# Four due times of a hand-written timetable: a transform's first step by 0.14, the last transform by 0.12

## The chip, the cores and the metric

The kernel runs on one core of one Trainium2 chip. The metric is the device time of one execution in microseconds. The kernel before takes 3285.62 us, the median of three runs (3276.33 to 3288.96).

## The reference

The input is a batch of 32 images of 56 x 56 tokens with 96 channels, in float32. Two layers follow one another.

```python
# layer 0: layer norm over channels, product to 192, 3x3 convolution back to 96
h = (x - mu) * rsqrt(var + 1e-5) * ln_w + ln_b
x1, z = split(einsum('bhwc,cd->bhwd', h, w_in) + b_in, 2)
x = x + silu(conv3x3(x1, conv_w) + conv_b)
# layer 1: the 3136 tokens of an image mixed in the frequency domain
h = relu(bn1(einsum('bnc,hc->bnh', ln(t), w1)))
X = fft(h, axis=tokens)
xr = relu(X.real * rd - X.imag * idg + rb)
xi = relu(X.imag * rd + X.real * idg + ib)
t = t + bn2(einsum('bnh,ch->bnc', ifft(xr + 1j * xi).real, w2))
# and a two-layer network on values quantised to eight bits, accumulated in 16
t = t + q(relu(q(ln(t) @ W1.T + b1)) @ W2.T + b2)
```

## The kernel before

An image's 3136 tokens lie as 112 partitions of 28 tokens. They go in 7 groups of 4 tokens a partition (index g) or in four chunks of 8, 8, 8 and 4 (index i). The convolution works on a copy of the image in channels by position (make_image), with six combined rows in place of three (conv_part in three parts, conv_first, conv_last), and its output returns to tokens (conv_tokens, conv_end).

The Fourier transform of length 3136 = 112 x 28 is done in two steps. The first, over 112, is a matmul for each pair of tokens: tokens_a turns a group to channels, forth multiplies by w1 (tile ph, line 209, then the relu into tile h, line 212), forth_a applies the transform (tile pa, line 218, copied to tile u). store_a writes u to a scratch in DRAM, da, and fetch_a reads it back in another layout, tile at. The second step, over 28, is second (tile px, line 233, one matmul for each pair of frequencies; index m is one of four units of frequencies and u a part of the channels). Three activations of px give av (lines 238 to 240); second_parts makes sv on VectorE (lines 249 to 252) and second_relus makes gt (lines 258 and 259). The way back is second_w2 (tile pg), second_back (tile pe, copied to es), store_back (es to a second scratch, de), fetch_y (de to tile y), back (tile py, line 294) and back_end, which adds py to the tokens on VectorE (line 474) and, for every second group, takes the statistics of the next layer norm. The quantised network follows: normal, ffn_start, ffn_first three times (tile pf, line 305), ffn_middle (lines 315 and 316), ffn_second (tile po), ffn_end and store.

Work of several images runs at once. Each step of each image gets a due time in a timetable: plan(b) puts it at 8 * b plus a number, so that a new image starts every 8 units, and steps of several images interleave. The list is sorted by due time and the steps are emitted in that order. The program is built with a scheduler that follows the order of emission as a preference (line 848): each engine's own order is fixed when the program is built, from what the scheduler reckons to be ready, so a step can overtake one that is due earlier. On the chip each engine works through its own list, and an instruction that waits holds those behind it. All DMAs named here are issued from one queue, that of SP.

The PSUM tiles ph, px and py share one tag, "c", with two buffers (lines 207, 227 and 293); pa, pg, pe and po share another, "b", also with two. The tag "a" of pf has one.

The due times that matter, taken modulo 8 so that steps of neighbouring images stand beside each other: second(0, 0) of an image at 0.00; ffn_first(5, 1), of the image two before it, at 0.13; forth(0, 0) of the next image at 0.15; a part of its convolution, conv_part(2, 1), at 0.20; back(0) of the image before at 0.38; ffn_first(5, 2) at 0.41; forth_a(0, 0) at 0.42; conv_tokens(3) at 0.45; ffn_start(6) at 0.50; back_end(0) at 0.53; ffn_middle(5, 2) at 0.58; conv_end(3) at 0.60; second(0, 1) at 0.62. From line to line they come from these numbers of plan: FIRST for the first transform, BACK for the last one, FFN for the network; second has its own list of offsets (line 572), and fetch_y is due at the later of BACK - 0.6 and 2.9 before its back.

Of the kernel before, what the change touches and what calls it, by code (L numbers as in the profile page):

```python
# [80 lines left out]
def hybrid_kernel(ctx: ExitStack, tc: tile.TileContext, x, par, spar, w_in, conv_w, w1, w2, fw1, fb1, fw2, fb2, fa, fb, ib, ia, rows6, out):  # L81
# [437 lines left out]
    def plan(b):  # L519
        im = Image(b)  # L520

        def put(when, f, *args):
            order.append((8 * b + when, len(order), lambda: f(im, *args)))

        for i, (j0, j1) in enumerate(LN_CHUNKS):
            last = i == len(LN_CHUNKS) - 1

            at = CONV - 8 + 2 * (i + 1)
            ats = (-0.95, -0.7) if last else (0.2, 0.5, 0.85) if i == 2 else (0.25, 1.0, 1.5)
            put(at + ats[0] - (2.5 if b else 12), fetch, i)  # L530
            put(at + ats[0] - 1.15, take_in, i)
            for part, j in enumerate(range(0, j1 - j0, 3)):
                put(at + ats[part], make_image, i, j, min(3, j1 - j0 - j))

            at = CONV + 2 * i
            put(at + 0.6, im_load, i)
            ats = (0, 0.35, 0.7) if last else (0, 0.5, 1.25)
            for part in range(3):
                put(at + ats[part], conv_part, i, part)
            put(at + ats[1] + 0.2, conv_first, i)  # L540
            put(at + ats[2] + 0.2, conv_last, i)
            for g, off in zip(range(j0 // G4, j1 // G4), (1.85, 2.75)):
                put(at + off, conv_tokens, g)
                put(at + off + 0.15, conv_end, g)
            put(FIRST + 2 * i - 0.75, deviation, i)
        put(CONV - 0.6, make_seam)
        for g in range(NG):
            at = FIRST + g
            put(at - 0.35, tokens_a, g)
            for j2 in range(2):  # L550
                put(at + 0.15 + 0.6 * j2, forth, g, j2)
                put(at + 0.42 + 0.58 * j2, forth_a, g, j2)
            put(at + 1.2, store_a, g)
            at = BACK + g
            put(max(BACK - 0.6, at - 2.9), fetch_y, g)
            put(at, back, g)
            put(at + 0.15, back_end, g)
            at = FFN + g
            put(at - 0.7, normal, g, 0)
            put(at - 0.55, normal, g, 2)  # L560
            put(at - 0.35, ffn_start, g)
            for k in range(3):
                put(at + 0.28 * k, ffn_first, g, k)
                put(at + 0.28 * k + 0.17, ffn_middle, g, k)
            put(at + 1.0, ffn_second, g)
            put(at + 1.15, ffn_end, g)
            put(at + 1.5, store, g)
        for g in range(NS):
            put(max(FIRST + 7.4, g - (1.4 if g % 2 else 2.2)), fetch_a, g)
        for m, (p0, p1) in enumerate(UNITS):  # L570
            both = p1 - p0 > PG
            for at, u in ((0, 0), (0.62, 1), (1.25, 2)) if both else ((0, 0), (0.62, 2)):
                at += 2 * m
                put(at, second, m, u)
                put(at + 0.22, second_parts, m, u)
                put(at + 0.42, second_relus, m, u)
            for j0 in range(0, (p1 - p0) // 2, 2):
                at = 2 * m + (2 if both else 1.3) + 0.2 * j0
                put(at, second_w2, m, j0)
                put(at + 0.2, second_back, m, j0)  # L580
                put(at + 0.4, store_back, m, j0)
# [1 line left out]
    def im_load(im, i):  # L583
        im.load(i)

    CONV, FIRST, BACK, FFN = -12.3, -8, 8.38, 10.85
    for b in range(nb):
        plan(b)
    order.sort(key=lambda step: step[:2])
# [262 lines left out]
```

## Time and profile before

| what | value |
|---|---|
| median of three runs | 3285.62 us |
| the profiled execution | 3286.24 us |
| its span, first to last instruction | 3284.5 us |
| mean granted TensorE clock | 0.985 |
| TensorE matmul busy | 3178.5 us, 97% |
| VectorE busy | 2527.3 us, 77% |
| ScalarE busy | 2202.5 us, 67% |
| GpSimd busy | 573.4 us, 17% |
| issue to landing, median: da, at, de, y | 3.4, 4.7, 2.2, 2.8 us |

The profile is of one execution. Busy times are of each engine over the whole span. In the views of instructions each line is: start in us from the span's first instruction, duration in us, engine and line, operation, written tile and read tiles, shapes, how many were merged, and in brackets the idle time of the engine just ahead and what ended it. One matmul in float32 leaves two records. A row of the view of waits names an engine and line, what it waited for, the us in total, how many times, and the longest.

### The profile page before, as it was taken

The page shows a single profiled execution, that of the slowest core. Times are in us where ns is not written, and L with a number is a line of the kernel's source. Part 1 is how long each engine was busy: PE and PEld are TensorE (multiplying, and loading weights), DVE is VectorE, ACT ScalarE, POOL GpSimd, SP SyncE. Part 2 cuts the span into 40 slices and gives each one's busy share as a digit, 9 for nine tenths or more (in the row PEclk, how much of TensorE's full clock was granted, in tenths as well). Part 3 has the DMA queues.
Part 4 walks back from the last instruction along what each step waited for, and adds up shares of the span by engine and source line. Part 5 has one row for each costly group of instructions (what it writes and reads, how often), then busy time and mean ns, then how long its engine had stood idle before and what let it go on. Part 6 is the DMA issues. An engine that isn't in the chain of part 4 may idle for free.

```text
span 3284.5 us, 66741 instructions
## 1 busy us (share of the span) xinstructions
PE 3178.5 (97%) x23701; PEld 2732.7 (83%) x23701; DVE 2527.3 (77%) x7829; ACT 2202.5 (67%) x5232; POOL 573.4 (17%) x397
## 2 busy tenths in 40 slices
PE   7999999999999999999999999999999999999997
PEld 6888888888888888888888888888888888888875
DVE  4558777777878777877877777777777778777787
ACT  2566666766766666766666766667767666666776
POOL 1211111111211111112111111111111111121111
PEclk8999999999999999999999999999999999999997
DMA  4343334434344333344333344343344333443341
GB/s 109 94 116 98 104 110 123 120 99 112 94 118 120 109 107 105 106 117 119 111 102 109 107 117 123 96 112 104 110 123 119 100 103 101 120 118 99 104 117 55
DMA packets 334551, 355.45 MB, mean 108 GB/s; under 512 B 129304, under 2 KB 287400, under 8 KB 333992
## 3 DMA queue, kind: packets, MB, share of 16 engines
q1 hardware_dynamic: 332210, 349.01, 37.7%
q8 instruction: 188, 3.08, 0.4%
q10 hardware_dynamic: 2008, 2.17, 0.2%
q14 instruction: 145, 1.19, 0.1%
HBM read 196.93 MB, written 154.14 MB: 107 GB/s over the span
## 4 chain that ended last, share of the span: by engine, by line
PE 88%; DMA 7%; DVE 2%; ACT 1%; issue 1%; SPq 1%; POOL 0%; ACTq 0%; DVEq 0%; POOLq 0%
PE cv L164 22%; PE px L233 9%; PE pa L218 9%; PE ph L209 9%; PE im L153 7%; PE pg L276 5%; PE pe L286 5%; PE tp_n L146 5%; PE pg L272 5%; PE py L294 5%; PE pf L305 4%; PE po L322 3%; DMA de<-es 2%; PE st L196 2%; DMA at<-da 2%; DMA y<-de 1%
## 5 line engine op out<-in xcount | busy, mean ns | idle before, releaser
L164 PE MATMUL cv<-img,wv 97*96 97x224 f32 (+1 forms) x4608 | 882.4, 332 | 0.2
L164 PEld LDWEIGHTS cv<-img,wv 97*96 97x96 f32 x4608 | 662.0, 164 | 93.2 <-issue 11.2
L138 POOL TENSOR_TENSOR rs_c<-var_c,mhalf 112x8 f32<-112x8 f32 (+1 forms) x128 | 195.0, 1523 | 1679.7 <-DVE var_a L136 868.9
L212 ACT ACTIVATE h<-ph,rs_b 112x192 f32<-112x192 f32 x896 | 332.3, 429 | 177.5 <-PE ph L209 176.2
L233 PEld LDWEIGHTS px<-fb_sb,at 112*64 112x64 f32 (+1 forms) x3584 | 324.7, 165 | 132.7 <-issue 48.9
L233 PE MATMUL px<-fb_sb,at 112*64 112x112 f32 (+3 forms) x3584 | 381.9, 274 | 35.1 <-DMA at<-da 34.1
L307 ACT CAST h<-pf 128x448 f16<-128x448 f32 x672 | 363.8, 541 | 67.8 <-PE pf L305 64.5
L209 PE MATMUL ph<-w1a,n2t 97*112 97x192 f32 x1792 | 373.7, 328 | 4.1 <-DVE sv L252 2.8
L218 PE MATMUL pa<-h,fa_sb 112*112 112x384 f32 x896 | 365.6, 490 | 0.0
L138 POOL TENSOR_TENSOR rs_b<-var_b,mhalf 112x8 f32<-112x8 f32 (+1 forms) x128 | 190.4, 1488 | 984.7 <-DVE var_a L136 552.1
L153 PE MATMUL im<-rows_sb,xa 112*97 112x168 f32 x1792 | 325.2, 312 | 11.0 <-DVE xa L372 9.8
L488 DVE TENSOR_SCALAR xn<-t,st_c,rs_c 112x96 f32<-112x96 f32 x896 | 232.2, 325 | 111.3 <-POOL rs_c L138 108.7
L249 DVE SCALAR_TENSOR_TENSOR sv<-px,spar_sb,av 128x224 f32<-128x224 f32 (+2 forms) x352 | 153.4, 436 | 200.2 <-ACT av L240 199.3
L209 PEld LDWEIGHTS ph<-w1a,n2t 97*112 97x112 f32 x1792 | 290.7, 177 | 17.4 <-DVE sv L252 3.3
L153 PEld LDWEIGHTS im<-rows_sb,xa 112*97 112x97 f32 x1792 | 268.0, 167 | 43.2 <-issue 14.7
L219 ACT COPY u<-pa 112x384 f32<-112x384 f32 x448 | 215.4, 481 | 120.8 <-PE pa L218 111.5
L316 DVE CAST hq<-h 128x448 fp8e5<-128x448 f16 x672 | 257.9, 384 | 11.3 <-ACT h L313 5.4
L315 DVE TENSOR_SCALAR h<-h,b1q 128x448 f16<-128x448 f16 x658 | 215.4, 327 | 59.2 <-ACT h L307 54.4
L305 PE MATMUL pf<-n3t,w1q 96*128 96x448 fp8e5 x672 | 243.8, 363 | 9.6 <-ACT h L307 8.8
L276 PE MATMUL pg<-w2x,gt 128*112 128x96 f32 (+1 forms) x1792 | 251.6, 261 | 0.0
L238 ACT ACTIVATE av<-px,spar_sb 128x224 f32<-128x224 f32 (+2 forms) x352 | 156.7, 445 | 135.3 <-PE px L233 132.5
L276 PEld LDWEIGHTS pg<-w2x,gt 128*112 128x112 f32 (+1 forms) x1792 | 242.7, 179 | 0.2
(115 smaller groups left out, 6148.1 us busy)
## 6 DMA issues: line engine op xcount, KB each, us to landing
da<-u SPq DMA_DIRECT2D x224, 336.0 KB, 3.4
at<-da SPq DMA_DIRECT2D x224, 336.0 KB, 4.7
de<-es SPq DMA_DIRECT2D x448, 84.0 KB, 2.2
y<-de SPq DMA_DIRECT2D x224, 168.0 KB, 2.8
out<-o SPq DMA_DIRECT2D x224, 168.0 KB, 2.4
xl<-in_x SPq DMA_DIRECT2D x96, 336.0 KB, 3.4
x<-in_x SPq DMA_DIRECT2D x96, 336.0 KB, 4.1
xl<-in_x SPq DMA_DIRECT2D x32, 168.0 KB, 2.3
```

Of the source, the lines that this page charges most:

```text
L138: nc.gpsimd.tensor_tensor(rs, var, mhalf[:, :n], ALU.pow)
L153: nc.tensor.matmul(ps[:, j], xa[:, j, :], rows6_sb, start=True, stop=True)
L164: nc.tensor.matmul(ps[:, at], wv[:, k, dx, :], cols, start=(dx == 0), stop=(dx == 2))
L209: nc.tensor.matmul(ph[:, j, :], n2t[:, 2 * j2 + j, :], w1a, start=True, stop=True)
L212: nc.scalar.activation(h[:, j], ph[:, j], AF.Relu, scale=rs[:, 2 * j2 + j : 2 * j2 + j + 1])
L218: nc.tensor.matmul(pa, fa_sb, h, start=True, stop=True)
L233: nc.tensor.matmul(px[rows, j], lhs, fb_sb[:, first(p) : first(p + 1)], start=True, stop=True)
L276: nc.tensor.matmul(pg[:, half, j, :], lhs, w2x, start=False, stop=True, skip_group_check=True)
L305: nc.tensor.matmul(pf, w1q[:, k * 128 : (k + 1) * 128], n3t, start=True, stop=True)
L307: nc.scalar.copy(h1, pf)
L316: nc.vector.tensor_copy(hq[:, k, :], h2, saturate=False)
L488: nc.vector.tensor_scalar(xc[:, j], im.t[i][:, at, :C], mu[:, at : at + 1], rs[:, at : at + 1], ALU.subtract, ALU.mult)
```

## The change

Two numbers of plan change. second(0, 0) of each image, with its second_parts and second_relus, is due 0.14 later (the other second steps stay). BACK goes from 8.38 to 8.5, so that every back, back_end and fetch_y of every image is due 0.12 later. No instruction is added, removed or altered.

```diff
             for at, u in ((0, 0), (0.62, 1), (1.25, 2)) if both else ((0, 0), (0.62, 2)):
-                at += 2 * m
+                at += 2 * m + (0.14 if m + u == 0 else 0)
                 put(at, second, m, u)
                 put(at + 0.22, second_parts, m, u)
                 put(at + 0.42, second_relus, m, u)
@@
-    CONV, FIRST, BACK, FFN = -12.3, -8, 8.38, 10.85
+    CONV, FIRST, BACK, FFN = -12.3, -8, 8.5, 10.85
```

## The prediction

> **What bounds the kernel now.** I read first the page's busy times and its chain, then the waits of TensorE, then TensorE, the DMA queue and VectorE instruction by instruction around one image boundary (1306 to 1334 us). From the page:
>
> ```profile
> PE 3178.5 (97%) x23701; PEld 2732.7 (83%) x23701; DVE 2527.3 (77%) x7829; ACT 2202.5 (67%) x5232; POOL 573.4 (17%) x397
> ...
> PE 88%; DMA 7%; DVE 2%; ACT 1%; issue 1%; SPq 1%; POOL 0%; ACTq 0%; DVEq 0%; POOLq 0%
> ```
>
> TensorE is busy for 97% and carries 88% of the chain; the other thing in the chain is DMA, 7%. So only two things can move the time: TensorE's work, which the change leaves as it is, and the stalls between. TensorE's waits, longest first (total us, times, longest):
>
> ```profile
> PE px L233 <- DMA at<-da: 34.1, 32, 2.5
> PE py L294 <- DMA y<-de: 15.6, 18, 2.5
> ...
> PE py L294 <- ACT n2t L202: 2.7, 6, 0.5
> ```
>
> One px wait an image (34.1 us in all). The py waits come to 21.2 us over 28 times with the smaller rows of py (named for ScalarE work that had long ended, so I put them to y as well). TensorE at one boundary (start us, us, idle before):
>
> ```profile
> 1309.08 0.58 PE L164 MATMUL cv<-img,wv 97*96 97x224 f32 x2
> 1310.71 1.15 PE L233 MATMUL px<-fb_sb,at 112*128 112x114 f32 x8 [1.04 <-DMA at<-da]
> 1311.69 0.35 PE L305 MATMUL pf<-n3t,w1q 96*128 96x448 fp8e5 x1
> 1311.89 0.81 PE L209 MATMUL ph<-w1a,n2t 97*112 97x192 f32 x4
> 1312.54 2.06 PE L164 MATMUL cv<-img,wv 97*96 97x224 f32 x10
> 1314.43 0.49 PE L196 MATMUL st<-ident,s 96*112 96x96 f32 x4
> 1314.76 0.55 PE L146 MATMUL tp_n<-ident,t 112*97 112x112 f32 x4
> 1315.15 0.35 PE L305 MATMUL pf<-n3t,w1q 96*128 96x448 fp8e5 x1
> 1316.05 0.87 PE L294 MATMUL py<-y,ia_sb 113*112 113x384 f32 x2 [0.55 <-DMA y<-de]
> 1316.76 0.81 PE L218 MATMUL pa<-h,fa_sb 112*112 112x384 f32 x2
> ```
>
> These are second(0, 0) of one image (the px line) and back(0) of the image before it (the py line): exactly the steps that move. Between them stand one ffn_first, a forth, ten of the twelve records of a conv_part (a float32 matmul leaves two), a conv_tokens, a tokens_a and another ffn_first. The next boundary's px starts at 1409.70, so 8 units of the timetable are 98.99 us and one is 12.4 us: +0.14 is 1.7 us and +0.12 is 1.5 us. The order shown is the same at every boundary from 711 to 2903 us. In the DMA queue:
>
> ```profile
> 1306.91 1.26 SPq L428 DMA_DIRECT2D at<-da  x3
> 1308.26 0.88 SPq L459 DMA_DIRECT2D de<-es  x2
> 1313.63 1.25 SPq L465 DMA_DIRECT2D y<-de  x3
> ```
>
> Both chains (da to at, de to y) begin with TensorE work that stands before px, so the two arrival times don't depend on where px and py stand.
>
> [...]the 84 KB of de land in 2.2 us at the median, the 336 KB of at in 4.7[...]. [...]here both bubbles name a DMA. [...]in the dense stretch each next start lies 0.16 before the end shown, so the true stalls are 0.16 longer than the brackets (1.20 and 0.71 above). [...]whatever stands behind a waiting px or py waits too.
>
> **The change, part by part.** No instruction is added or removed.
>
> *Due time and place.* A due time is a preference, not a place: ffn_start(6), due at 0.50, runs before px, due at 0.00. But the tiles px, ph and py share two PSUM buffers, and their first matmuls start in the timetable's order all 1,024 times. Their due order (px 0.00, ph 0.15, py 0.38, px 0.62) becomes 0.14, 0.15, 0.50, 0.62: the same. So neither step can pass a ph or another px.
>
> *second(0, 0), +0.14.* The only TensorE step due between 0.00 and 0.14 is ffn_first(5, 1), at 0.13; now it stands right behind px. If it goes ahead, 0.20 us (1311.69 to 1311.89) fill part of the px stall of 1.20. But py then waits for y at the same moment, 1316.05, and the work between is the same set: TensorE is back 0.20 earlier and waits 0.20 longer. Worth 0 where y is late, up to 0.20 where it is not. Its three av activations (0.45 to 0.54 each) and three sv operations pass at most the h and hq of ffn_first(5, 1) (0.33 + 0.38 on VectorE), and the gt pair passes conv_first's; px's buffer may come free some 0.7 later. Who waits for it is the next px, 1317.45, against sv's end at 1314.43: 3.0 us of cover. I cost it at nothing; without the cover it is 0.7 an image. gt's first reader is second_w2 at 2.00, twenty us on.
>
> *back, +0.12 (seven an image).* It passes ffn_first(5, 2) at 0.41 and conv_tokens and ffn_start at 0.45 and 0.50, which run ahead already, and forth_a(0, 0) at 0.42: the pa line, which stands right behind py. Was pa ready? Its h ended at 1314.27 (0.76 from 1313.51 on ScalarE), 1.8 before py. Why was it not ahead, then? In the planner's order py and pa come as a pair: at back(0), (1), (3) and (5) the next matmul is that image's pa, at each of 24 boundaries that I went through. py(1) there waits for no DMA. What py (a free buffer) and pa (its input) share is the end of the h activations, which free ph's buffer and complete h; so I take it that both become ready at once and the due time decides. 0.42 against 0.38 put pa second; against 0.50 it is first. The price of pa is 1317.41 - 1316.76 = 0.65 us, in a stall of 0.71: gain 0.65 here. Summed, with min(0.65, bracket + 0.16) for each of the 25 py stalls over 0.3 between 312 and 3006 us: 20 at 0.65, and 0.64, 0.61, 0.54, 0.53, 0.48: 15.8 us. The other boundaries had no py stall. At (1), (3) and (5) the swap is worth 0: no stall there.
>
> *back_end, +0.12.* On VectorE it passes behind ffn_middle at .58 and, for g = 0, 2 and 6, conv_end at .60 (0.56 + four times 0.27 + 0.16 = 1.8 us); for g = 1 take_in at 1.60. This holds py's buffer longer. The next ph(0, 1) starts 3.8 us after the t of back_end(0): cover. The tightest is g = 1, in the rivals.
>
> *fetch_y, +0.12.* On the DMA queue the only step passed is fetch_a(2), 7.80: the first three fetch_y are due at 7.90 instead of 7.78. The three at already run ahead (1306.91 against 1313.63), and y waits for de till 1313.6. Nothing; if it were issued behind one more at, 0.4 us. The later y fetches pass no other DMA. A fetch_y(5) that waits for py(1), now 0.65 later, holds the queue by as much: its y is needed 50 us later.
>
> *Tail.* The last image has no successor whose pa could fill in; back stands alone. 0, at most 1.5 us.
>
> Sum: 3286.24 (3284.5 span + 1.74 around it) - 15.8 = 3270.4. The profiled execution lies 0.62 above the median, so 3269.8 there; I say 3270.
>
> **The rivals.**
> - *Nothing changes (3286).* If pa becomes ready in the planner's eyes only while py runs (up to 0.65 later also gives the order seen), py stays ahead; moving px alone is worth nothing. For it: px's stall stays, since hardly anything is due before 0.14. Against it: the pairing at four places.
> - *Both waits go (3236).* If the planner's order also closes the px stalls, 34.1 + 32 x 0.16 = 39, and with 15.8 some 55, less 5 for the first and the last image: 3236; with half of px's, 3253. Against it: conv_part's rest (0.20) and ph (0.15) are still due after px.
> - *A held buffer makes it slower (3313).* Place: back(1). Its t runs on VectorE at 1332.28 to 1332.83, though py ended at 1328.98, and the px that needs the buffer, second(1, 0), starts 0.29 later. VectorE, then TensorE:
>
> ```profile
> 1332.28 0.55 DVE L474 TENSOR_TENSOR t<-py,t 112x384 f32<-112x384 f32 x1
> ```
>
> ```profile
> 1328.17 0.81 PE L294 MATMUL py<-y,ia_sb 113*112 113x384 f32 x2
> 1328.82 0.81 PE L218 MATMUL pa<-h,fa_sb 112*112 112x384 f32 x2
> ...
> 1333.12 1.04 PE L233 MATMUL px<-fb_sb,at 112*128 112x112 f32 x8
> ```
>
>  The delay of t lies between 0.38 (only the hq of ffn_middle and a var slip ahead: 0.30 + 0.08; the statistics of take_in run ahead already) and 2.06 (pa 0.65, ffn_middle 0.71, take_in 0.70). Less 0.29, TensorE stands 0.1 to 1.8 us an image: 3 to 55 us over 31, or 3273 to 3325 with the gain. It decides from a delay of 1.33 on, a net loss of 16 us; the middle of what lies above is 3313. Against it: TensorE has other work, and the planner can put it ahead of px.
>
> **How the numbers follow.** pa ahead of py: 0.43, 3262 to 3279 alone. Nothing changes: 0.20, 3280 to 3292. Both waits: 0.13, 3236 to 3262. Slower: 0.24, 3302 to 3325. 0.5% is 16.4 us, about what a measurement of this kernel can tell (three runs of it spread over 12.6): faster is below 3269.2, slower above 3302. The likeliest case stands at that edge; with the spread I count 0.19 of its 0.43 as faster. Faster 0.19 + 0.13 = 0.32, same 0.24 + 0.20 = 0.44, slower 0.24. Range 3246 to 3318: it leaves out some 0.06 below and 0.08 above.
>
> **What would show it.** In the changed trace pa should stand before py at the boundary, and py's brackets for y fall from 21.2 to about 6 us; px's stay near 34. ffn_first before px with the px bracket at 0.84 and py's longer would bear out the fixed arrival. The prediction is wrong if py still comes first, if a new wait (px L233 for a VectorE t at second(1, 0)) appears, or if at or y land at another distance from the px before.

## The result and the profile after

The changed kernel takes 3246.83 us (3242.14 to 3251.24, four runs) against 3284.72 for the kernel before beside it: ratio 0.9888, 95% interval 0.9863 to 0.9912. That is 37.9 us less, where 14 to 16 were forecast; it lies 0.8 us above the foot of the range (3246). The profiled execution has a span of 3245.6 us, 38.9 below the one shown before.

The page of the changed kernel, busy times and chain by engine:

```profile
PE 3167.5 (98%) x23701; PEld 2737.2 (84%) x23701; DVE 2529.4 (78%) x7829; ACT 2196.2 (68%) x5232; POOL 598.2 (18%) x397
...
PE 87%; DMA 7%; DVE 3%; ACT 1%; issue 1%; SPq 0%; POOL 0%; ACTq 0%; DVEq 0%; POOLq 0%
```

The instruction counts are the same to the last one, and DMA still has its 7%: nothing was saved in work. TensorE's waits in the changed kernel (us in total, times, longest):

```profile
PE px L233 <- DMA at<-da: 19.3, 27, 2.7
...
PE py L294 <- DMA y<-de: 8.3, 15, 2.0
```

Both waits fell: py's from 21.2 us (all its rows) to 8.7, and px's for at, which was expected to stay near 34, to 19.3. TensorE at one boundary of the changed kernel (start us, us, idle before):

```profile
2569.45 0.78 PE L153 MATMUL im<-rows_sb,xa 112*97 112x168 f32 x4
2570.07 0.26 PE L146 MATMUL tp_n<-ident,xn 112*96 112x112 f32 x1
2570.16 0.54 PE L164 MATMUL cv<-img,wv 97*96 97x224 f32 x2
2570.96 1.15 PE L233 MATMUL px<-fb_sb,at 112*128 112x114 f32 x8 [0.25 <-DMA at<-da]
2571.94 0.82 PE L209 MATMUL ph<-w1a,n2t 97*112 97x192 f32 x4
2572.59 0.35 PE L305 MATMUL pf<-n3t,w1q 96*128 96x448 fp8e5 x1
2572.79 2.06 PE L164 MATMUL cv<-img,wv 97*96 97x224 f32 x10
2574.68 0.49 PE L196 MATMUL st<-ident,s 96*112 96x96 f32 x4
2575.01 0.45 PE L146 MATMUL tp_n<-ident,xn 112*96 112x112 f32 x3
2575.30 0.81 PE L218 MATMUL pa<-h,fa_sb 112*112 112x384 f32 x2
2576.41 0.90 PE L294 MATMUL py<-y,ia_sb 113*112 113x384 f32 x2 [0.30 <-DMA y<-de]
```

pa stands before py, as forecast. But px has no more work ahead of it than before: the same single matmul of the convolution (two records) stands in front, and ffn_first went behind ph instead of ahead of px. Its wait is shorter because at came sooner. The DMA queue at that boundary:

```profile
2561.03 0.33 SPq L364 DMA_DIRECT2D xl<-in_x  x1
...
2564.45 0.30 SPq L422 DMA_DIRECT2D da<-u  x1
2567.32 1.25 SPq L428 DMA_DIRECT2D at<-da  x3
```

From the last da store to the first at it is 2.87 us here. In the kernel before, the load xl of 336 KB was issued 0.65 us ahead of that store and the at followed 3.60 us after it; here the load is 3.4 us ahead. Followed through the boundaries of images 4 to 28 (means, before and after, us):

| stretch | before | after |
|---|---|---|
| end of the last pa of an image to the issue of its da | 1.48 | 1.29 |
| that issue to the first at | 3.85 | 3.12 |
| first at to px | 3.60 | 3.63 |
| sum, from pa to px | 8.93 | 8.04 |
| bracket of px | 1.10 | 0.49 |
| TensorE work between (sum less bracket less 0.16) | 7.67 | 7.39 |
| end of the last pe to py, the y chain | 9.22 | 8.01 |

The chain to px is 0.89 shorter and the work between is 0.28 less, so 0.61 of the wait is gone. The y chain is shorter as well: de is issued behind the three at, and these go out sooner. Three of the 25 boundaries before had y landed well ahead of py, so that the 9.22 is not all chain; without them it is 8.98, and the chain is about 1.0 shorter.

Where the 37.3 us went that 24 periods (from px of image 4 to px of image 28) became shorter: px stalls 13.2, py stalls 10.6, other stalls -1.0; 7.0 in the part of a period without stalls, 97.11 us before and 96.82 after (the median of a period less its stalls); and the remaining 7.5 mostly in slow stretches of TensorE, at a granted clock of 0.50, that the kernel before has four times and the changed one not at all in these periods. The last two are taken up below. Ahead of these periods 1.0 us was gained, behind them 0.6.

### The profile page after: what moved, and what is told of

The parts are those of the page before. It is cut to its first block, busy times and chain, and to the rows that moved or that the text cites. A ratio compares the mean times of both kernels' runs of the same rounds, so it can differ in the third digit from the quotient of the medians.

```text
span 3245.6 us, 66513 instructions
## 1 busy us (share of the span) xinstructions
PE 3167.5 (98%) x23701; PEld 2737.2 (84%) x23701; DVE 2529.4 (78%) x7829; ACT 2196.2 (68%) x5232; POOL 598.2 (18%) x397
## 4 chain that ended last, share of the span: by engine, by line
PE 87%; DMA 7%; DVE 3%; ACT 1%; issue 1%; SPq 0%; POOL 0%; ACTq 0%; DVEq 0%; POOLq 0%
PE cv L164 21%; PE px L233 9%; PE ph L209 9%; PE pa L218 8%; PE im L153 7%; PE tp_n L146 5%; PE pg L276 5%; PE pe L286 5%; PE pg L272 5%; PE py L294 4%; PE pf L305 4%; PE po L322 4%; DMA de<-es 2%; PE st L196 2%; DMA at<-da 2%; DMA y<-de 1%
## 5 line engine op out<-in xcount | busy, mean ns | idle before, releaser
L164 PEld LDWEIGHTS cv<-img,wv 97*96 97x96 f32 x4608 | 671.3, 164 | 101.0 <-issue 16.4
L233 PE MATMUL px<-fb_sb,at 112*64 112x112 f32 (+3 forms) x3584 | 378.2, 273 | 21.7 <-DMA at<-da 19.3
L209 PE MATMUL ph<-w1a,n2t 97*112 97x192 f32 x1792 | 380.2, 329 | 3.3 <-DVE sv L252 2.0
L153 PE MATMUL im<-rows_sb,xa 112*97 112x168 f32 x1792 | 333.4, 312 | 11.3 <-DVE xa L372 10.1
L322 PEld LDWEIGHTS <-hq 128*112 128x112 fp8e5 x2688 | 198.5, 135 | 51.7 <-DVE hq L316 16.9
```

The costliest lines, as they stand in the source:

```text
L153: nc.tensor.matmul(ps[:, j], xa[:, j, :], rows6_sb, start=True, stop=True)
L164: nc.tensor.matmul(ps[:, at], wv[:, k, dx, :], cols, start=(dx == 0), stop=(dx == 2))
L209: nc.tensor.matmul(ph[:, j, :], n2t[:, 2 * j2 + j, :], w1a, start=True, stop=True)
L233: nc.tensor.matmul(px[rows, j], lhs, fb_sb[:, first(p) : first(p + 1)], start=True, stop=True)
L322: nc.tensor.matmul(po[:, j, :], hq[:, k, j * N1 : (j + 1) * N1], w2q[:, k, :], start=(k == 0), stop=(k == 2))
```

## The experiments

One table for all runs, in us an image over those 24 periods; 0.16 is added to each bracket; px and py are all stalls of those lines, whatever they wait for. What is missing to the period is mostly slow stretches. Ratios are of the timed runs, to the kernel before on the same chip. The other columns are each read from one execution, and chips differ: the kernel before took 3277.77, 3283.74, 3284.72 and 3287.57 us at the median on them. The runs named r repeat a kernel.

The expectations name their theories by letters: Q says that px waits less because the last da store no longer follows right behind a load, P because px itself is due later; S that the swap of pa and py is the whole gain; D is told after e3.

| run | ratio, 95% | period | px | py | other stalls | without stalls |
|---|---|---|---|---|---|---|
| before | 1 | 99.56 | 1.27 | 0.78 | 0.01 | 97.11 |
| changed | 0.9888 (0.9863 to 0.9912) | 98.01 | 0.72 | 0.34 | 0.05 | 96.82 |
| r1_changed_again | 0.9891 (0.9871 to 0.9911) | 98.01 | 0.80 | 0.20 | 0.03 | 96.85 |
| e1_second | 0.9964 (0.9950 to 0.9977) | 99.02 | 0.68 | 0.89 | 0.09 | 97.49 |
| e2_back | 0.9926 (0.9907 to 0.9945) | 97.89 | 0.58 | 0.42 | 0.05 | 96.82 |
| e3_py_only | 0.9860 (0.9843 to 0.9876) | 97.81 | 0.83 | 0.01 | 0.01 | 96.96 |
| r2_py_again | 0.9869 (0.9852 to 0.9887) | 97.91 | 0.85 | 0.04 | 0.06 | 96.94 |
| e4_no_swap | 0.9940 (0.9919 to 0.9960) | 98.39 | 0.56 | 0.43 | 0.18 | 97.23 |
| e9_back_alone | 0.9934 (0.9916 to 0.9953) | 98.84 | 1.41 | 0.07 | 0.02 | 97.14 |
| e10_py_sec014 | 0.9947 (0.9932 to 0.9963) | 98.92 | 1.37 | 0.16 | 0.00 | 97.27 |
| e6_second_021 | 0.9922 (0.9900 to 0.9944) | 98.70 | 0.00 | 0.62 | 0.75 | 97.30 |
| e8_py_sec021 | 0.9781 (0.9767 to 0.9796) | 96.85 | 0.01 | 0.01 | 0.03 | 96.78 |
| e5_half_load | one run, 3321.34 us | 100.48 | 0.54 | 1.68 | 0.52 | 97.38 |
| e7_after_half | one run, 3269.60 us | 99.07 | 0.21 | 0.15 | 0.66 | 98.02 |

### Each half alone

e1_second, from the kernel before:

```diff
-                at += 2 * m
+                at += 2 * m + (0.14 if m + u == 0 else 0)
```

> Only second(0, 0) is due 0.14 later; BACK stays at 8.38. The order that the program fixes at the boundary: py stands before pa as in the kernel before; the 336 KB load xl is still issued close before the last da store, with one out store between. Theory Q (px's wait shrank because the last da store is no longer issued right behind a load, so da lands about 0.7 us sooner; py's wait shrank because pa went ahead): nothing of either is here, px waits near 1.0 us an image, py near 0.6, ratio 1.000 (0.996 to 1.004), 3285 us. Rival P (px's wait shrank because px itself is due later): px waits halve as in the changed kernel, 34 to about 19 us in all, ratio 0.994.

Measured: 0.9964, at the edge of theory Q's range. px's waits for at fell to 20.1 us in all, the number of rival P. That rival's reason is not confirmed: the work between the last pa and px stayed (7.67 to 7.62 us), and the chain became 0.63 shorter, most of it because u was copied sooner at every other boundary (pa to da 1.02 on the mean, alternately 0.54 and 1.53). Most of what px gained, 0.59 an image, was given back: py's stall rose by 0.11, and the part without stalls by 0.38.

e2_back, from the kernel before:

```diff
-    CONV, FIRST, BACK, FFN = -12.3, -8, 8.38, 10.85
+    CONV, FIRST, BACK, FFN = -12.3, -8, 8.5, 10.85
```

> Only BACK goes to 8.5; second(0, 0) stays due at 0.00. The order at the boundary on TensorE and in the DMA queue is that of the changed kernel. Theory Q: all of the gain is in this half, ratio 0.989 (0.986 to 0.992), 3248 us, px waits near 19 us in all and py's near 9. Rival P: px's wait returns to 34 us, only the py part of the gain stays, ratio 0.995.

Measured: 0.9926, a period of 97.89 us, px's waits 17.0 us in all. Rival P, which had px's wait back at 34, is out. From 0.75 ms to 3.1 ms of the trace each engine and the DMA queue run their instructions in the very order of the changed kernel: once BACK has moved, the 0.14 of second(0, 0) changes the order only in the first images and at the end. So BACK alone makes the changed kernel's periods. By the timed runs it has two thirds of the gain; the two intervals overlap by a little, this trace is the fastest of its four runs, and what the 0.14 adds to BACK, between nothing and 0.4%, is left open.

### Only py later, and the swap undone

e3_py_only, from the kernel before (back_end and fetch_y stay):

```diff
-            put(at, back, g)
+            put(at + 0.05, back, g)
```

> The kernel before with back alone due 0.05 later (behind forth_a at 0.42), back_end and fetch_y as they were. In the program pa stands before py, and the load xl still stands right before the last da store. Theory Q: py's wait falls from 21 to about 9 us in all, px's stays near 34; with a few us of clock that is 3270 us, ratio 0.995 (0.992 to 0.998). Rival S (the swap of pa and py is the whole gain): ratio 0.989.

Measured: 0.9860, and 0.9869 again in r2_py_again: a larger gain than theory Q (0.995), rival S (0.989) or the whole changed kernel (0.9891 beside the repeat). py's waits are down to 2.8 us, where theory Q had about 9, and px's fell too, with the time from the da store to at hardly shorter (3.75 us). TensorE's waits over the whole run:

```profile
PE px L233 <- DMA at<-da: 18.3, 18, 3.4
...
PE px L233 <- DVE sv L252: 6.0, 10, 1.5
```

The planner put 8.26 us of work between the last pa and px instead of 7.67: 9.25 at every other boundary, where px never waits, and 7.3 at those between. What VectorE adds, in the table's 0.83 too, lies in mid-image. So theory Q, that the load is the reason, fails here: a stall is the chain less the work that the planner puts beside it, and either can move. I call that theory D from here on. As arithmetic it holds by definition; as a forecast it also needs the right guess of both terms.

e4_no_swap, from the changed kernel:

```diff
-            put(at, back, g)
+            put(at - 0.09, back, g)
```

> The changed kernel with back due at 8.41 in place of 8.5 (before forth_a again), back_end and fetch_y as in the changed kernel. In the program py stands before pa, and the load xl stands before the last da store with one out store between. Theory Q: py's wait is back near 20 us in all, px's near 30, ratio 0.999 (0.995 to 1.003). Rival P: px's wait stays near 19, ratio 0.994. Rival S: 1.000.

Measured: 0.9940. py stands before pa again, and yet its stall is 0.43, not 0.78, and px's 0.56: in this order the u copy runs at once (pa to da 0.54 us at every boundary), the chain is 7.44 us, and y follows sooner with it. Theory Q and rival S missed. Rival P had the ratio, and px's waits for at (16.0 us) near its 19, but e2 and e10 speak against its reason.

### The swap with the rest nearly in place

e9_back_alone, from the kernel before; TensorE's fixed order differs from the kernel before least of all runs, and the part without stalls is the same (97.14):

```diff
-            put(at, back, g)
+            put(at + 0.12, back, g)
```

> The kernel before with back alone due 0.12 later; back_end, fetch_y and second(0, 0) as before. In the program pa(0, 0) stands before py(0), ten of twelve steps around them as before, and the load xl is issued behind the last da store instead of ahead of it. Theory D (a wait is the length of the transfer chain less the TensorE work planned between its start and its reader; a load of 336 KB issued shortly ahead of the da store makes it land later): the time from the da store to the first at falls from 3.85 to about 3.0 us, px's stall from 1.27 to about 0.5 us an image, py's from 0.78 to about 0.2, ratio 0.987 (0.984 to 0.990). Rival S (only the swap counts): px's stall stays near 1.2, ratio 0.993.

Measured: 0.9934, which is 21.7 us (15.5 to 27.6) of 3287.57. Waits of TensorE:

```profile
PE px L233 <- DMA at<-da: 39.7, 31, 2.9
...
PE py L294 <- DMA y<-de: 2.8, 4, 1.2
```

py's wait fell from 21.2 to 2.8 us, while px's for at rose from 34.1 to 39.7: the planner put 7.30 us of work between the last pa and px instead of 7.67. This is the nearest to the prediction's main step by itself: 18.4 us of waits at py, where it summed 15.8. The 21.7 us are not this step alone: px's waits took 5.6 back, and slow stretches cost about 4.6 less. Theory D's guess on the da store failed: the load was issued 0.4 us behind the store instead of 0.65 ahead, and at still came only 3.64 us later. Rival S had the ratio, and px's stall (1.41 for its 1.2) nearer.

Against e2 this kernel leaves back_end and fetch_y where they were, and nothing else differs. px's waits are 39.7 us here and 17.0 there, so the due times of these two steps are part of what shortened px's wait. The ratios, 0.9934 and 0.9926, don't tell the two apart.

e10_py_sec014 is the kernel before with back 0.05 and second(0, 0) 0.14 later:

```diff
-            put(at, back, g)
+            put(at + 0.05, back, g)
...
-                at += 2 * m
+                at += 2 * m + (0.14 if m + u == 0 else 0)
```

> The kernel before with back due 0.05 later and second(0, 0) 0.14 later. In the program pa stands before py, the other steps between px and py are those of the kernel before, ffn_first goes inside px, and the load xl is issued behind the last da store. Theory D: as with back alone 0.12 later: px's stall 1.2 to 1.4, py's near 0.1 us an image, ratio 0.993 (0.991 to 0.996). Rival P (the later due time of second(0, 0) itself shortens px's stall): px's near 0.7, ratio 0.988.

Measured: 0.9947, px's stall 1.37, py's 0.16, as theory D had it. Here the 0.14 stands with pa already ahead of py, and px's stall did not shorten: the later due time alone is not what shortens it.

### What sets the landing of da

Both kernels use two buffers for the loads of xl instead of three, so that the chunk loaded ahead of the last da store is the small one:

```diff
-        tag, bufs = ("xn", 2) if im.b == 0 and i == 3 else ("xl", 3)
+        tag, bufs = ("xn", 2) if im.b == 0 and i == 3 else ("xl", 2)
```

e5_half_load does so in the kernel before, e7_after_half in the changed one.

> The kernel before with two buffers in place of three for the loads xl: the load that is issued ahead of the last da store is then the chunk of 168 KB, not one of 336 KB. Theory D: from the da store to the first at about 3.4 us on the mean, against 3.85. Rival (the landing of da does not depend on the load ahead of it): 3.8.

> The changed kernel with two buffers for the loads xl: a load of 168 KB is then issued close ahead of the last da store, where the changed kernel has none within 3 us. Theory D: from the da store to the first at about 3.4 us on the mean, against 3.12, and px's stall longer by as much less what is planned between. Rival: 3.1.

Measured: da store to first at 3.41 us in e5 (expected 3.4), 2.96 in e7 (expected 3.4; the rival's 3.1 is nearer). e5 took 3321 us against 3288, with 1.68 us an image of waits at py; in e7 px's stall fell to 0.21, where theory D had it longer. Neither is a clean test, since other transfers moved too: in e7 the out store went behind da. The nearest pair is e4, with a load of 336 KB 2.2 us ahead and 3.40 us to at, and e7, with one of 168 KB 2.4 us ahead and 2.96. DMA in the stretch from the da store to at, kernel before, then changed (length in us; busy us and instructions of PE, PEld, DVE, ACT and POOL; clock, DMA share, GB/s):

```profile
1303.31:1306.91 3.60, 3.60 (x28) 3.29 (x27) 2.00 (x8) 1.77 (x4) 0.00 (x0) 1.00 0.83 239
```

```profile
2564.45:2567.32 2.87, 2.87 (x22) 2.54 (x20) 2.60 (x9) 0.91 (x2) 0.00 (x0) 1.00 0.61 170
```

The DMA engines move 239 GB/s x 3.60 us = 860 KB (thousands of bytes) before at goes, against 170 x 2.87 = 488 KB in the changed kernel. Over the 25 boundaries the packets that ended from store to at were 862 KB before and 516 after, of which da has 344. So my estimate from these counts is that da lands later the more bytes are in flight beside it, issued ahead of it or behind. Most runs fit: 489 to 524 KB go with 2.96 to 3.19 us, 649 KB (e4) with 3.40, 768 to 862 KB with 3.60 to 4.02, e9 (833 KB, 3.64 us) among them. e5 does not: 531 KB, 3.41 us. It is argued from the byte counts, not shown by a run that changes only them.

### More work ahead of px

e6_second_021, from the changed kernel, puts second(0, 0) behind forth and conv_part(2, 1):

```diff
-                at += 2 * m + (0.14 if m + u == 0 else 0)
+                at += 2 * m + (0.21 if m + u == 0 else 0)
```

> The changed kernel with second(0, 0) due 0.21 later instead of 0.14: in the program a forth and all of conv_part(2, 1) stand before px, 2.7 us of work, and pa, ffn_first and a transpose between px and py. Theory D: px's stall 0 and py's below 0.1 us an image, some 1 us an image less than in the changed kernel: ratio to the kernel before 0.980 (0.977 to 0.984), 3218 us. Rival B (the buffer that px, ph and py share is held longer and TensorE waits for VectorE instead): no faster than the changed kernel, ratio 0.988 or more.

Measured: 0.9922. Theory D's 0.980 missed. px's stall is 0.00, but TensorE stands elsewhere, as rival B warned, though not for VectorE: it waits for y and for ScalarE. Its waits:

```profile
PE py L294 <- DMA y<-de: 18.9, 19, 2.0
...
PE st L196 <- ACT s L191: 8.5, 26, 1.6
```

With px behind it, the conv_part that used to lie between px and py lies in front of both, and from px to py it is 3.0 us instead of 5.3: y, with a chain of its own, is now what TensorE waits for. st waits for the silu of the convolution.

e8_py_sec021 takes the 0.21 to the kernel of e3:

```diff
-            put(at, back, g)
+            put(at + 0.05, back, g)
...
-                at += 2 * m
+                at += 2 * m + (0.21 if m + u == 0 else 0)
```

> The kernel before with back due 0.05 later and second(0, 0) 0.21 later. In the program px has forth and all of conv_part(2, 1) ahead of it, and a conv_part stands between px and py, which comes behind pa. Theory D (a wait is the length of the transfer chain less the work planned between its start and its reader): px's and py's stalls both below 0.1 us an image, ratio 0.981 (0.978 to 0.985), the fastest so far. Rival C (as with second 0.21 later in the changed kernel, TensorE then waits for ScalarE, or the transfers come later): 0.986 or more.

Measured: 3210.47 us, 0.9781, the fastest of all, 35.8 us below the changed kernel beside it (3246.26). Waits of TensorE over the whole run:

```profile
PE py L294 <- DMA y<-de: 4.9, 4, 1.7
...
PE px L233 <- DMA at<-da: 4.2, 3, 2.8
```

These lie at the first and last images; within the 24 periods no stall is left to speak of, and a period is 96.85 us, of which 96.78 is TensorE without stalls. The planner put 9.9 us between the last pa and px, and a second conv_part between px and py (6.05 us). Theory D had this one.

r1_changed_again and r2_py_again:

> The changed kernel once more, beside the next on one chip: 0.9888 (0.986 to 0.992), px's stall near 0.7 and py's near 0.35 us an image. No theory differs on it.

> The kernel before with back alone due 0.05 later once more, beside the changed kernel on one chip: 0.986 (0.984 to 0.988), faster than the changed kernel by 0.3% (0.0 to 0.5%). No theory differs on it.

Both came out as expected, and the one-step kernel was the faster by 7.8 us in the medians.

## Why the prediction came out as it did

- **What bounds the kernel.** Right for the stalls: two DMA waits an image. e8 removes both and ends within 0.07 us of TensorE's time without stalls in a period. That TensorE's work stays as it is held for its instructions, not quite for their time (last point).
- **pa ahead of py, 15.8 us.** Right in mechanism and size. pa stands before py at all 25 boundaries in each of the ten traces with back due behind forth_a, and behind it in the other four, so the due time decides; 0.05 is enough. e9 has 18.4 us less wait at py for it. In the changed kernel itself py's waits fell by 12.5, not 15, with the y chain moved too.
- **"Both chains ... begin with TensorE work that stands before px, so the two arrival times don't depend on where px and py stand."** This is the step that failed. It holds for one fixed order. But a due time is a preference for the planner, and new due times gave a new order everywhere, the ScalarE copy of u, the loads and the de stores included. The chain to px became 0.89 us shorter (0.73 of it from the da store to at), the one to py about 1.0. px's waits for at, counted at no gain, fell by 14.8 us in all. The same 336 KB store let at go after 3.85 us before and after 3.12 in the changed kernel.
- **second(0, 0), "0 where y is late, up to 0.20".** ffn_first did not go ahead of px but behind ph. Alone the step gave 0.36%, by the shorter chain and not by the work ahead of px, which it did not raise; beside BACK it left the order of the periods as it was (e2).
- **back_end, fetch_y, tail at nothing.** Right in that no buffer was held: in the changed kernel px waited once for a VectorE t, for 0.6 us. fetch_y still waited for de (79.6 us over 39 waits of the DMA queue, 122.6 over 38 before), and from px of image 28 to the end it is 380.5 us against 381.1. Not right that their due times do nothing: e2 and e9 differ by those of back_end and fetch_y alone, and px's waits were 17.0 and 39.7 us.
- **The rivals.** "Nothing changes" and "a held buffer" are out. The time lies nearest to "both waits go" at half of px's (3253), which had 0.13. That rival left room for a re-plan, but weighed it only by work put ahead of px, and the rest of conv_part and ph still come after px; that the chain could become shorter had no term. The likeliest case, 3262 to 3279, did not come. That the result still lies inside the range, by 0.8 us, is luck: more than half of the gain came by ways that the sum did not have.
- **Two terms missed.** The part of a period without stalls became 0.29 us shorter, 7.0 us over 24 periods. It is 96.8 to 98.0 in the runs, with the same instructions in another order. Some of it (0.91 us a period before, 0.75 after) is gaps too short to count as stalls here; the rest is not settled. And some stalls are followed by a slow stretch, at a granted clock of 0.50, as the last section tells: 9.4 us in the kernel before.

## What to carry to other kernels

Where a planner fixes the order from due times, a small edit is not a local swap: the order that it would change must be read again for the whole period, on every engine and on the DMA queue, before the rest is held fixed. Of my own forecasts from such a reading, those for e5, e8 and e10 came true and those for e6, e7 and e9 did not. A stall on a transfer is the length of the chain from its start to its landing less the work that stands between (at the boundaries of the kernel before 8.93 us less 7.67 and 0.16, a bracket of 1.10), so look for the start of the chain as much as for work to put ahead of the waiting step. And filling one stall can empty the cover of the next: in e6 the same conv_part served px or py, not both (stalls of 0.00 and 0.62 us an image), and only the order with one for each (e8, 0.01 and 0.01) gained on both.

## What the runs showed of the hardware

Some stalls of TensorE are followed by a stretch in which its granted clock is 0.50. The kernel before, the wait of px at the boundary at 911 us, and the ten microseconds around it (columns as above; clock 0.66):

```profile
910.87 2.05 PE L233 MATMUL px<-fb_sb,at 112*128 112x114 f32 x8 [2.02 <-DMA at<-da]
```

```profile
908.00:918.00 10.00, 7.98 (x37) 6.64 (x35) 3.18 (x10) 3.69 (x10) 0.00 (x0) 0.66 0.75 206
```

The clock is 0.50 for 6.8 us, from 910.6 to 917.4, and 1.00 on either side. The same eight records of px take 2.05 us here and 1.15 at the boundary at 1311 us, at a clock of 1.00.

Between 200 and 3000 us the fourteen traces hold 24 such stretches, each of 3.4 or 6.8 us at 0.50. Each began 1.7 to 3.7 us after the start of an idle bracket of TensorE; the shortest of these brackets was 1.45 us (0.16 not added here). Of 53 brackets over 1.4 us, 24 were followed by one. In the kernel before it was four of nine: brackets of 2.02, 1.62, 2.45 and 1.45 us ahead of the stretches at 910.6, 1112.0, 2607.0 and 2805.0 us, while five of 1.80 to 2.01 us were not followed by any. So the length of the stall alone does not tell which are, and what does is not shown. One stretch of 3.4 us made its period 1.6 longer, one of 6.8 us 3.1: the kernel before lost 9.4 us so at four boundaries. That the stall is the cause is read from these coincidences; no run varied it by itself.
